# A triangle multiplication and a gated pair layer on one core: held pieces of b by channels eight apart, two output projections among the last products, the last block's factors on GpSimd

## The chip, the core and the metric

One NeuronCore of a Trainium2 chip runs the whole kernel. The metric is the device time of the program in microseconds (us); its time is the median of several executions. Engines are named as the profile names them: PE is the tensor engine (PEld its weight loads), DVE the vector engine, ACT the scalar engine, POOL is GpSimd, SP the engine whose queue issues most of the DMAs.

## The reference

Two layers over x of 384 x 384 positions with 128 channels, all in float32:

```python
# layer 0: triangle multiplication
z_n = layernorm(z)
a = linear(z_n, Wa, ba) * sigmoid(linear(z_n, Wga, bga))
b = linear(z_n, Wb, bb) * sigmoid(linear(z_n, Wgb, bgb))
x = einsum('bijd,bjkd->bikd', a, b)       # for each channel d a 384x384x384 product
x = layernorm(x)
pair = z + linear(x, Wo, bo) * sigmoid(linear(z_n, Wgo, bgo))
# layer 1: gated pair layer
left = pair @ W_left + b_left + (pair @ W_eq + b_eq)
right_sum = sum(pair @ W_right + b_right, over axis 2)
out = left * right_sum * sigmoid(pair @ W_gate + b_gate)
y = layer_norm(out @ W_out + b_out + pair)
```

## The kernel before

The schedule is manual: each engine's queue runs its instructions in the order in which the program writes them, so the order of the Python code is the order of the work. Tiles come from pools with a fixed number of buffers; an instruction that takes a buffer waits until its last readers are done. There are three stages, which hand their data on through DRAM.

**Stage 1, projections (to 1396.9 us).** The positions are cut into 72 tiles of 128 rows by 16 columns, and each tile into 4 steps of 4 columns. A step normalises z (ACT L160, with factors that POOL works out by a power of -0.5, L149), transposes it (zT), and makes a (pa, pga) and b (pb, pgb) with the channels on the partitions; a goes to DRAM array A from POOL's queue (L267), b to B from SP's queue. The output gate is projected by `gate_project` (PE L211 into pgo; DVE L213 adds the bias into one of three gs buffers; ACT L198, in `gate`, takes the sigmoid into one of two gt buffers; POOL issues the store to G, L201). The gate projections of the last 16 steps are put off to the end of the stage. The normalised input's residual Z is stored by POOL (L171 and its DMA). The last 64 columns of b for the last 128 rows are not stored at once: they stay in the SBUF tile `b_held` (channel = partition, 128 rows, 64 columns).

**Stage 2, products (1396.9 to about 2148 us).** For each channel d, `fetch` loads A[d] and B[d] (SP, L470) six channels ahead, `multiply` makes three blocks of 128 rows of the product in PSUM (tile pm, PE L488), and `product` takes the difference to channel 0 (DVE L500, xd), its square (ACT L505, sq), the sums s1 (POOL L507) and s2 (DVE L481), and stores xd to X (SP L508). `store_held` writes 16 channels of `b_held` at a time to B from SP's queue (L476): the first piece ahead of the first full loads, the second right after the loads of the first six channels, and the other six in the course of the stage. A few passes of products that do not need the held columns (`EARLY`) are done at once. The last 8 channels (`LAST`) are done block by block, so that the factors of a block's layer norm can be worked out by `deviation(ib)` between the next block's products: ACT L424, L428 and L432, DVE L426, L427, L430 (a reciprocal), L433, L435 and L437, then three transposes on PE (L443) and a copy on ACT (L444) into `rs0`. `deviation` is a generator, and `advance` runs it one step on. For the last block there is no next block: two steps of it run right after the last product and the others between the first rows of stage 3, the transposes (`pr_last`) in the pass u = 6.

**Stage 3, rows (to the end).** A loop over u writes the work of several rows per pass, each stage of the pipeline with a lag: `load(u+8)` in groups of four rows (xr from X, gr from G, zr from Z, all on SP's queue, L410 to L412), `gate_product(u-3)` (DVE L580), `turn(u-2)` (three transposes, PE L566 into ptr; ACT L568 copies to pairT), `out_weights(u-7)` (ACT L574), `layer_1(u-8)` (PE L592, pf), `layer_0(u)` (PE L602, py; DVE L608 multiplies by factors and gate, L615 adds zr and gives pair; DVE L613 and L618 take the statistics of row u-8), `norm_factors(u-12)` (POOL L625, L626 a power, L628, L629, once in four rows), `normalise(u-13)` (ACT L635), `project(u-2)` (PE L643 pleft and L645 pg; ACT L650 sigmoid; PE L656 once in four rows) and `store(u-17)` (POOL L674 and L675 on four rows at once, then the output's DMA).

## Time and profile before

| | us |
|---|---|
| median of 3 runs | 3340.28 (3338.49 to 3342.46) |
| the profiled execution | 3343.24 |
| its span, first to last instruction | 3341.5 |
| PE busy | 3293.7 (99%) |
| DVE, ACT, POOL busy | 2666.1, 2311.3, 2091.9 |
| mean granted clock of PE | 0.994 |

The profile is of one execution. PEclk is the clock granted to PE, as a share of full speed. A line number such as L488 is that of the code below. In a line of a timeline the bracket at the end gives how long the engine had stood idle, and which instruction's end released it.

### The profile page before, as it was taken

What the parts mean: (1) busy time and instruction counts of PE and PEld (TensorE: products, weight loads), DVE (VectorE), ACT (ScalarE), POOL (GpSimd) and SP (SyncE); (2) the same over time, 40 slices, a digit from 0 to 9 for tenths busy, and PEclk for the clock granted to TensorE, in tenths of its full rate; (3) what the DMA queues carried; (4) which work ended last, traced back from release to release, by engine and by line L of the source; (5) the groups of instructions that cost most, each with busy time, mean ns of one, the idle gap of its engine ahead of it and who ended that gap; (6) DMA issues with size and microseconds to landing.
All of it is one profiled execution on the core that took longest, in us unless ns stands there. A gap on an engine that the chain in (4) does not pass through costs nothing.

```text
span 3341.5 us, 53397 instructions
## 1 busy us (share of the span) xinstructions
PE 3293.7 (99%) x15581; PEld 2191.3 (66%) x15581; DVE 2666.1 (80%) x8599; ACT 2311.3 (69%) x5488; POOL 2091.9 (63%) x1574
## 2 busy tenths in 40 slices
PE   8999999999999999999999999999999999999997
PEld 5555555555555555555555555588888888888885
DVE  8877777777777777455555555799999999999998
ACT  7778787877777788522222222378888888888887
POOL 7555555555555555355555555358888888888887
PEclk9999999999999999999999999999999999999998
DMA  6889899889888889899999999767777777777774
GB/s 226 265 256 273 278 282 282 278 279 281 280 269 264 268 275 282 254 337 318 312 315 311 312 311 304 258 231 262 261 263 262 262 262 264 264 263 263 263 265 142
DMA packets 675522, 910.52 MB, mean 272 GB/s; under 512 B 319520, under 2 KB 616480, under 8 KB 647712
## 3 DMA queue, kind: packets, MB, share of 16 engines
q1 hardware_dynamic: 634192, 680.28, 63.9%
q0 software_dynamic: 40320, 226.51, 19.3%
q8 instruction: 126, 2.06, 0.2%
q14 instruction: 164, 1.34, 0.1%
q10 hardware_dynamic: 720, 0.33, 0.0%
HBM read 454.04 MB, written 452.98 MB: 271 GB/s over the span
## 4 chain that ended last, share of the span: by engine, by line
PE 96%; DVE 2%; POOL 1%; DMA 1%; ACT 0%; issue 0%; POOLq 0%; ACTq 0%; SPq 0%; DVEq 0%
PE pm L488 22%; PE pga L246 8%; PE pa L246 7%; PE pgb L246 7%; PE pb L246 7%; PE py L602 7%; PE pf L592 7%; PE pgo L211 7%; PE pleft L643 7%; PE pg L645 7%; PE ptr L180 4%; PE ptr L566 4%; DMA G<-gt 0%; DVE py L608 0%; PE pg L656 0%
## 5 line engine op out<-in xcount | busy, mean ns | idle before, releaser
L488 PE MATMUL pm<-ab 128*128 128x384 f32 x2304 | 746.6, 487 | 5.8 <-DVE gs L213 5.8
L488 PEld LDWEIGHTS pm<-ab 128*128 128x128 f32 x2304 | 438.9, 191 | 312.4 <-DVE gs L213 6.7
L507 POOL TENSOR_TENSOR acc<-acc,xd 128x384 f32<-128x384 f32 x381 | 380.1, 998 | 362.4 <-DVE xd L500 362.2
L505 ACT ACTIVATE sq<-xd 128x384 f32<-128x384 f32 x381 | 188.5, 495 | 542.3 <-DVE xd L500 542.2
L276 DVE SCALAR_TENSOR_TENSOR bt<-pb,c_L_conv_bb,sgb 128x512 f32<-128x512 f32 x288 | 320.9, 1114 | 243.3 <-ACT zT L191 218.6
L160 ACT ACTIVATE zn<-xt,off,rstd 128x128 f32<-128x128 f32 x1152 | 503.3, 489 | 2.9 <-POOL off L151 2.8
L635 ACT ACTIVATE res<-res,off,rs 128x128 f32<-128x128 f32 x1152 | 482.5, 486 | 18.4 <-POOL off L629 15.7
L500 DVE TENSOR_TENSOR xd<-pm,acc 128x384 f32<-128x384 f32 x381 | 212.2, 557 | 343.3 <-POOL acc L507 321.3
L608 DVE SCALAR_TENSOR_TENSOR py<-py,acc,gr 128x128 f32<-128x128 f32 x1152 | 433.7, 377 | 2.2 <-PE py L602 1.6
L267 POOL DMA_DIRECT2D A<-at x72 | 85.4, 1186 | 539.2 <-DVE at L263 539.2
L251 ACT ACTIVATE sga<-pga,c_L_conv_bga 128x512 f32<-128x512 f32 x288 | 197.9, 687 | 267.6 <-PE pga L246 267.6
L211 PEld LDWEIGHTS pgo<-wT_go,zT 128*128 128x128 f32 x2176 | 285.7, 192 | 130.0 <-issue 66.5
L613 DVE BATCH_NORM_STATS2 st<-res 128x6 f32<-128x128 f32 x1152 | 361.4, 315 | 0.3
L675 POOL TENSOR_TENSOR res<-res,r_L_conv_ln_bias 128x1536 f32<-128x1536 f32 x94 | 324.6, 3453 | 7.4
L171 POOL TENSOR_TENSOR acc<-xt,r_L_conv_b_out 128x2048 f32<-128x2048 f32 x72 | 327.4, 4548 | 1.8
L592 PE MATMUL pf<-w_o,h 128*128 128x128 f32 x2304 | 321.2, 276 | 6.1 <-ACT w_o L574 5.3
L674 POOL TENSOR_TENSOR res<-res,r_L_conv_ln_scale 128x1536 f32<-128x1536 f32 x94 | 325.3, 3461 | 0.2 <-issue 0.2
L650 ACT ACTIVATE sg<-pg,c_L_conv_b_gate 128x384 f32<-128x384 f32 x384 | 223.0, 581 | 144.5 <-PE pg L645 92.6
L602 PE MATMUL py<-w_o,xr 128*128 128x128 f32 x2304 | 321.1, 276 | 0.0
L643 PE MATMUL pleft<-pairT,m_L_conv_W_left 128*128 128x384 f32 x768 | 313.1, 489 | 2.8 <-ACT pairT L568 2.8
L645 PE MATMUL pg<-pairT,m_L_conv_W_gate 128*128 128x384 f32 x768 | 311.1, 487 | 0.0
L141 DVE BATCH_NORM_STATS2 st<-xt 128x6 f32<-128x128 f32 x1152 | 305.5, 265 | 3.7 <-DMA xt<-in_x_dram 3.6
(142 smaller groups left out, 6826.8 us busy)
## 6 DMA issues: line engine op xcount, KB each, us to landing
A<-at POOLq DMA_DIRECT2D x72, 1024.0 KB, 8.5
Z<-acc POOLq DMA_DIRECT2D x72, 1024.0 KB, 8.2
G<-gt POOLq DMA_DIRECT2D x72, 1024.0 KB, 9.2
xr<-X SPq DMA_DIRECT2D x96, 768.0 KB, 6.0
gr<-G SPq DMA_DIRECT2D x96, 768.0 KB, 7.6
zr<-Z SPq DMA_DIRECT2D x96, 768.0 KB, 8.8
X<-xd SPq DMA_DIRECT2D x381, 192.0 KB, 6.2
xt<-in_x_dram SPq DMA_DIRECT2D x71, 1024.0 KB, 17.9
```

The source lines that it names most:

```text
L160: nc.scalar.activation(g["zn"][:, c, :], g["x"][:, c, :], AF.Identity, bias=g["off"][:, c : c + 1], scale=g["rstd"][:, c : c + 1],)
L211: nc.tensor.matmul(pgo[:, c, :], lhsT=zT[:, c, :], rhs=wT["go"], start=True, stop=True)
L246: nc.tensor.matmul(pk, lhsT=wT[k], rhs=zT, start=True, stop=True)
L488: nc.tensor.matmul(products[d, ib], lhsT=ab[:, 0, q, ib * P : (ib + 1) * P], rhs=ab[:, 1, q, :], start=(q == 0), stop=(q == NB - 1),)
L507: nc.gpsimd.tensor_tensor(s1[:, ib, :], s1[:, ib, :], xd, ALU.add)
L592: nc.tensor.matmul(pf[:, q, :], lhsT=h[:, q * P : (q + 1) * P], rhs=w_o, start=True, stop=True)
L602: nc.tensor.matmul(py[:, q, :], lhsT=g["x"][:, i, q * P : (q + 1) * P], rhs=w_o0, start=True, stop=True)
L608: nc.vector.scalar_tensor_tensor(py[:, q, :], py[:, q, :], rs0[:, q, u : u + 1], g["g"][:, i, q, :], ALU.mult, ALU.mult)
L613: nc.vector.bn_stats(b["st"][:, k, q, :], b["res"][:, k, q, :])
L635: nc.scalar.activation(g["res"][:, i, q, :], g["res"][:, i, q, :], AF.Identity, bias=g["off"][:, i, q : q + 1], scale=g["rs"][:, i, q : q ...
L643: nc.tensor.matmul(pleft, lhsT=w_left, rhs=pairT, start=True, stop=True)
L645: nc.tensor.matmul(pg[:, 0:N], lhsT=w_gate, rhs=pairT, start=True, stop=True)
```

## The change

There are three parts.

1. The channels are taken in the order 0, 8, 16, ..., 120, 1, 9, ...: `order[d]` is the channel that is loaded and stored at place d. `store_held` writes the 16 channels k, k+8, ..., k+120 of `b_held`, so a piece stands on partitions eight apart instead of on 16 adjacent ones.
2. `load` is split into `load_pair` (gr, zr) and `load_x` (xr). For the first eight rows `load_pair` is issued among the last products of the second block, and `load_x` at the beginning of the last block. `layer_0(0)` and `layer_0(1)` are written after the third last and the second last product, with py in one of stage 2's pm banks. The row loop begins at u = 2.
3. The factors of the last block are made by `last_deviation` on POOL: five operations on 128 x 384, then the power of -0.5 in 48 pieces of 128 x 8, then a product for X and the transposes. One step is written in each pass for u = 2 to 11, and from then on one in each pass with u % 4 = 1: pieces to u = 181, the product and its store at u = 185, the transposes at u = 189. Rows 256 and on use these factors. DVE's and ACT's operations of `deviation` are left for the first two blocks.

```diff
-    def deviation(ib, bank):
+    def load_x(u):
+        xr = pl.tile([P, R, N], FP, tag="xr", name=f"xr_{u}")
+        u1 = u % P
+        nc.sync.dma_start(out=xr, in_=X[u // P][:, u1 : u1 + R, :])
+        group[u // R]["x"] = xr
...
+    def deviation(ib):
...
+    def turn_factors(ib, r, pr):
         for q in range(NB):
             nc.tensor.transpose(pr[:, q * P : (q + 1) * P], r[:, q * P : (q + 1) * P], ident)
         nc.scalar.copy(rs0[:, :, ib * P : (ib + 1) * P], pr.rearrange("p (q i) -> p q i", q=NB))
+
+    def last_deviation(ib, bank):
+
+        v, t, r = (work_of.tile([P, N], FP, tag="w" + k, name=f"{k}_{ib}") for k in "vtr")
+        nc.gpsimd.tensor_tensor(t, s1[:, ib, :], s1[:, ib, :], ALU.mult)
+        yield
+        nc.gpsimd.tensor_scalar(t, t, -1.0 / (C * C), None, ALU.mult)
+        yield
+        nc.gpsimd.tensor_scalar(v, s2[:, ib, :], 1.0 / C, None, ALU.mult)
+        yield
+        nc.gpsimd.tensor_tensor(v, v, t, ALU.add)
+        yield
+        nc.gpsimd.tensor_scalar(v, v, 0.0, EPS, ALU.max, ALU.add)
+        yield
+        W = 8
+        for k in range(0, N, W):
+            nc.gpsimd.tensor_tensor(r[:, k : k + W], v[:, k : k + W], mhalf[:, 0:W], ALU.pow)
+            yield
+        nc.gpsimd.tensor_tensor(t, v, r, ALU.mult)
+        nc.sync.dma_start(out=X[ib][0], in_=t)
+        yield
+        turn_factors(ib, r, bank())
...
+        order = [d for k in range(C // HELD) for d in range(k, C, C // HELD)]
...
-                    out=factors[d][:, k, q0:q1], in_=of[d, q0 * P : q1 * P].rearrange("(q p) i -> p q i", p=P)
+                    out=factors[d][:, k, q0:q1],
+                    in_=of[order[d], q0 * P : q1 * P].rearrange("(q p) i -> p q i", p=P),
...
-        def store_held(d):
-            if d < C:
-                nc.sync.dma_start(out=B[d : d + HELD, N - P :, N - CG :], in_=b_held[d : d + HELD])
+        def store_held(i):
+            if i < C:
+                k = i // HELD
+                nc.sync.dma_start(out=B[k :: C // HELD, N - P :, N - CG :], in_=b_held[k :: C // HELD])
...
-            nc.sync.dma_start(out=X[ib][d], in_=xd)
+            nc.sync.dma_start(out=X[ib][order[d]], in_=xd)
...
         for ib in range(NB):
-            if ib == NB - 1:
-                load(0)
-                load(R)
             for d in range(C - LAST, C):
+                if ib == NB - 1 and d == C - LAST:
+                    load_x(0)
+                    load_x(R)
                 product(d, ib)
                 if behind:
                     advance(behind)
+                if ib == NB - 2 and d in (C - LAST, C - LAST + 1):
+                    load_pair((d + LAST - C) * R)
+                if ib == NB - 1 and d in (C - 3, C - 2):
+                    layer_0(d + 3 - C, -1, lambda u: pp2.tile([P, N], FP, tag="pm", name=f"py_{u}").rearrange(
+                        "p (q c) -> p q c", q=NB
+                    ))
             add_squares()
-            behind = deviation(
-                ib, lambda b: pt2.tile([P, N], FP, tag="pr", name=f"pr_{b}")
-                if b < NB - 1 else pp.tile([P, N], FP, tag="ptr", name="pr_last")
-            )
-        advance(behind, 2)
+            behind = deviation(ib) if ib < NB - 1 else None
...
-        for u in range(N + stages[-1][1]):
+        load(2 * R)
+        behind = last_deviation(NB - 1, lambda: pp.tile([P, N], FP, tag="ptr", name="pr_last"))
+        for u in range(2, N + stages[-1][1]):
             for stage, lag in stages:
                 if stage is layer_0:
-                    stage(u, u - 8)
+                    stage(u, u - 8, lambda u: pyp.tile([P, NB, C], FP, tag="py", name=f"py_{u}"))
                 elif 0 <= u - lag < N or (stage is last_right and u - lag == N):
                     stage(u - lag)
-            advance(behind)
+            if u < 12 or u % R == 1:
+                advance(behind)
```

More of the change, by code (lines that the diff above doesn't have):

```diff
@@ L405, in load, with load_pair @@
             return
-        xr = pl.tile([P, R, N], FP, tag="xr", name=f"xr_{u}")
+        load_pair(u)
+        load_x(u)
+    def load_pair(u):
         zr = pl.tile([P, R, NB, C], FP, tag="zr", name=f"zr_{u}")
         gr = pl.tile([P, R, NB, C], FP, tag="gr", name=f"gr_{u}")
-        u1 = u % P
-        nc.sync.dma_start(out=xr, in_=X[u // P][:, u1 : u1 + R, :])
         nc.sync.dma_start(out=gr, in_=G[u : u + R].rearrange("i (p q) c -> p i q c", q=NB))
         nc.sync.dma_start(out=zr, in_=Z[u : u + R].rearrange("i (p q) c -> p i q c", q=NB))
-        g = {"x": xr, "z": zr, "g": gr}
+        g = {"z": zr, "g": gr}
         g["total"] = pl.tile([P, R], FP, tag="total", name=f"total_{u}", bufs=4)
@@ L416, in load, with of, layer_0 @@
         group[u // R] = g
-    def deviation(ib, bank):
+    def load_x(u):
[3 more added lines that the diff above has]
+        group[u // R]["x"] = xr
+    def of(u):
+        return group[u // R], u % R
+    pairs = {}
+    def layer_0(u, v, bank):
+        now, past = 0 <= u < N, 0 <= v < N
+        if now:
+            g, i = of(u)
+            py = bank(u)
+            for q in range(NB):
+                nc.tensor.matmul(
+                    py[:, q, :], lhsT=g["x"][:, i, q * P : (q + 1) * P], rhs=w_o0, start=True, stop=True
+                )
+            pairs[u] = pairs_of.tile([P, NB, C], FP, tag="pair", name=f"pair_{u}")
+        for q in range(NB):
+            if now:
+                nc.vector.scalar_tensor_tensor(
+                    py[:, q, :], py[:, q, :], rs0[:, q, u : u + 1], g["g"][:, i, q, :], ALU.mult, ALU.mult
+                )
+            if past:
+                b, k = of(v)
+                nc.vector.bn_stats(b["st"][:, k, q, :], b["res"][:, k, q, :])
+        if now:
+            nc.vector.tensor_tensor(pairs[u], py, g["z"][:, i], ALU.add)
+        if past:
+            for q in range(NB):
+                nc.vector.bn_aggr(b["mv"][:, k, q, :], b["st"][:, k, q, :])
+    def deviation(ib):
         def work(k):
@@ L440, in deviation @@
         yield
-        pr = bank(ib)
+        turn_factors(ib, r, pt2.tile([P, N], FP, tag="pr", name=f"pr_{ib}"))
+    def turn_factors(ib, r, pr):
         for q in range(NB):
@@ L532 @@
         pl = ctx.enter_context(tc.tile_pool(name="p3l", bufs=3, reuse_waits="tile"))
+        pairs_of = ctx.enter_context(tc.tile_pool(name="p3r", bufs=12, reuse_waits="tile"))
         behind = None
         for ib in range(NB):
-            if ib == NB - 1:
-                load(0)
-                load(R)
             for d in range(C - LAST, C):
+                if ib == NB - 1 and d == C - LAST:
+                    load_x(0)
+                    load_x(R)
                 product(d, ib)
@@ L556 @@
     ) as pp:
-        pairs, hs, wos = {}, {}, {}
-        def of(u):
-            return group[u // R], u % R
+        hs, wos = {}, {}
         def turn(u):
@@ L593, in layer_1 @@
             nc.vector.tensor_tensor(g["res"][:, i], pf, pairs.pop(u), ALU.add)
-        def layer_0(u, v):
-            now, past = 0 <= u < N, 0 <= v < N
-            if now:
-                g, i = of(u)
-                py = pyp.tile([P, NB, C], FP, tag="py", name=f"py_{u}")
-                for q in range(NB):
-                    nc.tensor.matmul(
-                        py[:, q, :], lhsT=g["x"][:, i, q * P : (q + 1) * P], rhs=w_o0, start=True, stop=True
-                    )
-                pairs[u] = ps.tile([P, NB, C], FP, tag="pair", name=f"pair_{u}", bufs=12)
-            for q in range(NB):
-                if now:
-                    nc.vector.scalar_tensor_tensor(
-                        py[:, q, :], py[:, q, :], rs0[:, q, u : u + 1], g["g"][:, i, q, :], ALU.mult, ALU.mult
-                    )
-                if past:
-                    b, k = of(v)
-                    nc.vector.bn_stats(b["st"][:, k, q, :], b["res"][:, k, q, :])
-            if now:
-                nc.vector.tensor_tensor(pairs[u], py, g["z"][:, i], ALU.add)
-            if past:
-                for q in range(NB):
-                    nc.vector.bn_aggr(b["mv"][:, k, q, :], b["st"][:, k, q, :])
         def norm_factors(u):
```

## The prediction, written before the changed kernel had run

> **What bounds the kernel now.** First the busy times and the chain of waits of the whole page.

> ```profile
> PE 3293.7 (99%) x15581; PEld 2191.3 (66%) x15581; DVE 2666.1 (80%) x8599; ACT 2311.3 (69%) x5488; POOL 2091.9 (63%) x1574
> ...
> PE 96%; DVE 2%; POOL 1%; DMA 1%; ACT 0%; issue 0%; POOLq 0%; ACTq 0%; SPq 0%; DVEq 0%
> ```

> TensorE is busy 3293.7 of 3341.5 us and holds 96% of the chain that ended last. An edit can shorten the run only where PE stands idle or runs below full clock. Taking the span window by window (columns: length, then PE, PEld, DVE, ACT, POOL busy with counts, PEclk, DMA share, GB/s), I find three such places: the two borders between stages, and the last 40 us.

> ```profile
> 1383.00:1387.00 4.00, 4.00 (x38) 4.00 (x37) 3.04 (x6) 2.85 (x5) 0.30 (x1) 1.00 0.93 248
> 1387.00:1391.00 4.00, 4.00 (x38) 4.00 (x37) 3.19 (x5) 2.19 (x4) 0.81 (x2) 1.00 0.60 77
> ...
> 1403.00:1407.00 4.00, 4.00 (x7) 2.19 (x8) 0.69 (x1) 2.19 (x4) 0.93 (x2) 0.50 1.02 353
> ```
> ```profile
> 2150.00:2160.00 10.00, 4.26 (x12) 3.06 (x13) 8.79 (x18) 4.16 (x8) 1.02 (x2) 0.64 0.99 345
> 2160.00:2170.00 10.00, 9.53 (x44) 6.84 (x42) 7.87 (x18) 3.66 (x10) 0.00 (x0) 0.85 0.42 137
> ...
> 2500.00:2560.00 60.00, 60.00 (x391) 48.70 (x390) 60.00 (x241) 52.80 (x146) 49.37 (x31) 1.00 0.77 264
> ```

> The stretch 2500-2560 stands for stage 3: PE and DVE both full, POOL not. The timeline at the border of stages 1 and 2 (start, us, engine, line, [idle before <-releaser]) names the cause:

> ```profile
> 1399.53 2.19 ACT L198 ACTIVATE gt<-gs 128x512 f32<-128x512 f32 x4 [9.55 <-DMA G<-gt]
> 1400.19 2.48 DVE L213 TENSOR_TENSOR gs<-pgo,r_L_conv_bgo 128x512 f32<-128x512 f32 x4 [8.19 <-ACT gt L198]
> ...
> 1402.73 1.65 PE L488 MATMUL pm<-ab 128*128 128x384 f32 x2 [5.77 <-DVE gs L213]
> ```

> A product needs a PSUM bank that DVE's gate addition (L213) empties; that waits for a gs buffer, released by ACT's sigmoid (L198); that waits for a gt buffer, released when a G store lands. The two G stores were issued at 1386.70 and 1390.27 and took up to 12.8 us; the page's median for G is 9.2. Beside them only 77 GB/s moved, with the first held store on SP's queue (issued 1382.62, landed 14.9 us later). PE loses 5.77 us idle, and then until about 1408.65 works at PEclk 0.50: nine passes at 0.64 instead of 0.32 us, 2.9. **Together 8.7 us.**

> At the border of stages 2 and 3:

> ```profile
> 2154.21 2.54 DVE L430 RECIPROCAL r<-sg 128x384 f32<-128x384 f32 x1
> ...
> 2154.35 0.90 PE L566 MATMUL ptr<-ident,pair 128*128 128x128 f32 x3 [4.67 <-DVE pair L615]
> ...
> 2156.78 0.52 ACT L432 ACTIVATE t<-r 128x384 f32<-128x384 f32 x1 [3.53 <-DVE r L430]
> 2157.21 0.56 ACT L568 ACTIVATE pairT<-ptr,c_L_conv_b_out 128x384 f32<-128x384 f32 x1
> ...
> 2157.92 1.65 PE L643 MATMUL pleft<-pairT,m_L_conv_W_left 128*128 128x384 f32 x2 [1.39 <-ACT pairT L568]
> ```

> PE waits 4.67 us for the first pair. Then the last block's factors stand ahead of the rows: ACT waits for the reciprocal, and PE for ACT, 1.39. PE is at half clock till about 2162.9; ptr of row 2 comes at 2164.09.

> [...] The held piece is 64 floats = 256 bytes a row[...] the trace shows G slow there, not why.[...]

> **The change, part by part.**

> (1) Held pieces eight apart. A piece has the same 2048 rows of 256 bytes[...] The G stores come free that much earlier and the first lands near 1396 instead of 1399.5; the page's median for G says the same (1386.70 + 9.2 = 1395.9). PE resumed 3.2 us after that landing (ACT, DVE, PE in a row), which gives 1399.1. Its own work lasts until 1396.96, so it waits some 2.2 us; the bank that follows the second landing may add 0.5[...].[...] **Gain 8.7 - 2.2 = 6.5** (5.5 to 8; 3.6, the idle alone, if the clock drops all the same; 0 if the store is not faster). Its later pieces go out during stage 2, where PE is full and loads have six channels of lead: nothing. The channel order alone moves no work: A and B loads, products and X stores are the same in number and size.

> (2) Rows 0 and 1 early. py_0 and py_1 (six passes, 1.5 us) move from after the last product into the last three, PE's total unchanged. Their DVE work goes ahead of the last xd: 3 x 0.38 + 0.56 each. Pair 0 is ready about 2150.0, pair 1 about 2152.6. The first transpose's PSUM bank, however, is freed by the addition of squares of the last product but one, which now stands behind these: about 2153.65. So PE's idle stays near 4.1 us, and I take the clock drop as happening (85%). What does go is the reciprocal chain (L426 to L437), and with it the 1.39 us before pleft. From ptr_0 to ptr_1 6.29 - 1.39 = 4.9 us at half clock: ptr_1 at 2158.55. The other restart was at half clock for 5.9 us, so mine ends near 2159.6, and ptr_2, in the chain of 2.79 us a row seen right after, comes at 2161.0 instead of 2164.09. **Gain 3.1** (2.4 to 3.7; 1.5 if half clock lasts as long as before; 5.2 with no drop). The early g and z loads go on SP's queue during the second block's last products; xr for rows 0 to 7 stays before the last block (issued 2134.56, py_0 needs it at about 2144, an xr load takes 6.0): nothing. pr_last with its 1.21 us of PE (0.49 and 0.71 idle on ACT's copy) moves from row 6 to row 189: nothing net.

> (3) The last factors on GpSimd. Rows 2 to 11 take five prelude operations and five pow pieces of 128x8; POOL is at 0.00 in 2160-2170: nothing. The other 43 pieces go one to a group of four rows, rows 13 to 181. What POOL has there:

> ```profile
> L675 POOL TENSOR_TENSOR res<-res,r_L_conv_ln_bias 128x1536 f32<-128x1536 f32 x6 | 20.7, 3453 | 0.5
> L674 POOL TENSOR_TENSOR res<-res,r_L_conv_ln_scale 128x1536 f32<-128x1536 f32 x5 | 17.3, 3461 | 0.0
> L626 POOL TENSOR_TENSOR rs<-rs,mhalf 128x12 f32<-128x12 f32 x5 | 11.5, 2298 | 0.4
> ...
> L625 POOL TENSOR_SCALAR rs<-mv 128x12 f32<-128x12 f32 x5 | 1.2, 248 | 9.0 <-DVE mv L618 9.0
> ```

> A group takes 12.01 us (4 x 2.96 and one L656). POOL's six operations with gaps take 10.3; it waits 9.0/5 = 1.8 before L625. The same pow at 128x8 appears in stage 1 (L149) at 1.67 us, with a gap 1.75: 12.05 against 12.01. POOL falls behind by about 0.04 a group, 43 x 0.04 = 1.7 us at the most; its reader, ACT's L635, waited on POOL only 15.7 us in the whole run, so ACT has slack of its own. **Loss 0.3** (0 to 4). DVE, full here, is not slowed by a busier POOL: L608 took 3 x 0.38 with POOL idle at 2165 and 377 ns on the mean of all rows. DVE's six operations of the last factors are those that (2) takes away; no new wait is put on DVE or ACT, and at row 189 on PE only pr_last's.

> **Sum:** -6.5 - 3.1 + 0.3 = -9.3. The profiled execution took 3343.24 us (span 3341.5), 2.96 above the median 3340.28; 3343.24 falls to 3333.9, the median to **3331.0**. About 0.2%, 6.7 us, is what a measurement of this kernel can tell from no change.

> **Rivals.** *The held store is no faster*[...]. For: 2048 packets of 256 bytes either way, and DMA share is 0.60, not full, while they go.[...] Gain 3.1 - 0.3: 3340.28 - 2.8 = 3337.5, no change to be told. This is also the case that the change does not do what it says. *The clock drops at both borders although PE waits less*: part 1 gives 3.6, part 2 1.5: 3340.28 - 4.8 = 3335.5.[...] *No drop anywhere*: 8.0 + 5.2 - 0.3: 3327.4.[...] against: 4.67 dropped it. *GpSimd becomes the bound of rows 13 to 181*: slower. Each group grows by what a piece exceeds 1.7 us; the price is 43 times the excess, and the point is 0.38 us: 43 x 0.38 = 16.3 eats the 9.6 of the other parts and 6.7 more. A piece of 2.2 us gives 43 x 0.5 = 21.5, so 3340.28 - 9.6 + 21.5 = 3352.2. For: the margin of 0.05 us is nil, and PE, DVE and POOL would all be full. Against: 1.67 is measured on this operation and shape.

> **Chances.** Forecast 0.50, drop at both 0.10 (all of it within 0.2%), no drop 0.10, store no faster 0.18, GpSimd 0.12. Faster: 0.50 + 0.10 = 0.60; same 0.10 + 0.18 = 0.28; slower 0.12. The range runs from just under the best case, 3326.0, to 3345, which takes in the store's failure together with a loss of 4 on GpSimd (3341.2) and the mild end of the slower case; the rest of that, under 0.12, is left out.

> **What would show it.** Right: over 120 GB/s in the windows that had 77, G landing in about 8 us, PE's wait among the first products about 2 us and PEclk never at 0.5 there; ptr of row 0 about 0.7 us earlier, pairT of row 0 right behind it; L625's wait near nothing in rows 13 to 181 and rows still 12.0 us in four; an idle of 0.7 us near row 189. Wrong: G still landing after 12 us; a group of 12.4 us while the pieces run; PE's idle at the second border over 5 us.

## The result and the profile after

The changed kernel takes 3332.67 us (median of 11 runs, 3331.92 to 3333.19); the kernel before, beside it, 3341.18 (11 runs, 3338.49 to 3343.26). The ratio is 0.9975, with a 95% interval of 0.9968 to 0.9983: 8.5 us faster. The prediction said 3331.0, 9.3 us faster. The profiled execution has a span of 3330.9 us against 3341.5 before, 10.6 less; some 2 us of that are the kernel before's own, whose profiled execution (3343.24) lies 2.1 above its median.

The page of the changed kernel, busy times and chain of waits:

```profile
PE 3289.1 (99%) x15581; PEld 2188.5 (66%) x15581; DVE 2661.4 (80%) x8593; ACT 2309.9 (69%) x5485; POOL 2178.3 (65%) x1628
...
PE 97%; DVE 1%; POOL 1%; ACT 0%; DMA 0%; issue 0%; POOLq 0%; ACTq 0%; DVEq 0%
```

PE has the same 15581 instructions and 4.6 us less busy time, which fits passes that ran at half clock before and run at full clock now. POOL's busy time rose by 86.4 us, and the span did not follow it. Code lines have moved: L488 is now L554, L566 is L632, L568 is L634, L643 is L684, L625 is L666.

**The first border.** Windows of the changed kernel (length, busy PE, PEld, DVE, ACT, POOL, PEclk, DMA share, GB/s), then its timeline:

```profile
1387.00:1391.00 4.00, 4.00 (x38) 4.00 (x37) 2.99 (x6) 2.52 (x4) 0.86 (x2) 1.00 0.82 202
...
1399.00:1403.00 4.00, 4.00 (x12) 2.23 (x13) 0.69 (x1) 2.17 (x4) 1.12 (x2) 1.00 1.03 379
```
```profile
1387.13 0.56 POOL L201 DMA_DIRECT2D G<-gt  x1 [4.73 <-ACT gt L198]
...
1395.72 2.19 ACT L198 ACTIVATE gt<-gs 128x512 f32<-128x512 f32 x4 [5.31 <-DMA G<-gt]
...
1398.92 23.34 PE L554 MATMUL pm<-ab 128*128 128x384 f32 x71 [1.54 <-DVE gs L213]
```

Where 77 GB/s moved, 202 do. G's first store, issued at 1387.13, lets the sigmoid go at 1395.72, 8.6 us later; before, it was 12.8. The first held store itself lands after 9.7 us instead of 14.3. PE idles 1.54 us instead of 5.77, and after that PEclk is 1.00, not 0.50. In this execution the border costs 1.54 instead of 8.7 us.

**The second border.** Timeline of the changed kernel:

```profile
2147.13 0.90 PE L632 MATMUL ptr<-ident,pair 128*128 128x128 f32 x3 [4.02 <-DVE acc L547]
...
2148.07 0.58 ACT L634 ACTIVATE pairT<-ptr,c_L_conv_b_out 128x384 f32<-128x384 f32 x1 [0.52 <-PE ptr L632]
...
2149.11 1.28 PE L684 MATMUL pleft<-pairT,m_L_conv_W_left 128*128 128x384 f32 x2
...
2150.87 0.49 PE L632 MATMUL ptr<-ident,pair 128*128 128x128 f32 x3
```

PE still idles 4.02 us ahead of the first transpose, and the releaser is as predicted the addition of squares (L547), not the pair. The first transposes run at half clock (0.90 for three); pairT follows directly, pleft waits for nothing, and the next transposes at 2150.87 are at full clock (0.49). I measure this border from the end of the work that both orders have done by then (products, pr, py of rows 0 and 1) to the first transpose of row 2: 2149.68 to 2164.09 before, 14.4 us; 2143.11 to 2153.66 after, 10.55. That is 3.9 us less.

**The rows.** POOL's groups in 2500-2560 of the changed kernel (count, busy, mean ns, idle before):

```profile
L500 POOL TENSOR_TENSOR r<-v,mhalf 128x8 f32<-128x8 f32 x5 | 8.3, 1670 | 0.0
...
L666 POOL TENSOR_SCALAR rs<-mv 128x12 f32<-128x12 f32 x5 | 1.3, 257 | 0.8 <-DVE mv L453 0.8
```

A piece takes 1670 ns, and the wait for DVE fell from 9.0 to 0.8 us in five groups. PE is busy 60.00 of 60.00 in this window, as before. From ptr of row 2 to the last instruction it is 1177.4 us before (2164.09 to 3341.5) and 1177.2 after (2153.66 to 3330.9), so the pieces cost the rows nothing. At row 189 the predicted 0.71 us is there: the transpose behind pr_last has `[0.71 <-ACT acc L483]`, as row 6 had.

### The profile page after: what moved, and what is told of

Same layout as the page of the kernel before. It is cut to its first block, busy times and chain, and to the rows that moved or that the text cites. A ratio compares the mean times of both kernels' runs of the same rounds, so it can differ in the third digit from the quotient of the medians.

```text
span 3330.9 us, 53440 instructions
## 1 busy us (share of the span) xinstructions
PE 3289.1 (99%) x15581; PEld 2188.5 (66%) x15581; DVE 2661.4 (80%) x8593; ACT 2309.9 (69%) x5485; POOL 2178.3 (65%) x1628
## 4 chain that ended last, share of the span: by engine, by line
PE 97%; DVE 1%; POOL 1%; ACT 0%; DMA 0%; issue 0%; POOLq 0%; ACTq 0%; DVEq 0%
PE pm L554 22%; PE py L437 8%; PE pf L658 8%; PE pga L246 8%; PE pleft L684 7%; PE pg L686 7%; PE pa L246 7%; PE pgb L246 7%; PE pb L246 7%; PE pgo L211 7%; PE ptr L632 4%; PE ptr L180 4%; PE pg L697 0%; DMA G<-gt 0%; POOL rs L667 0%
## 5 line engine op out<-in xcount | busy, mean ns | idle before, releaser
L554 PE MATMUL pm<-ab 128*128 128x384 f32 x2304 | 744.1, 486 | 1.5 <-DVE gs L213 1.5
L554 PEld LDWEIGHTS pm<-ab 128*128 128x128 f32 x2304 | 437.3, 190 | 306.4 <-DVE gs L213 2.7
L676 ACT ACTIVATE res<-res,off,rs 128x128 f32<-128x128 f32 x1152 | 482.3, 486 | 14.3 <-POOL off L670 11.4
L566 DVE TENSOR_TENSOR xd<-pm,acc 128x384 f32<-128x384 f32 x381 | 212.1, 557 | 340.9 <-POOL acc L573 321.3
L443 DVE SCALAR_TENSOR_TENSOR py<-py,acc,gr 128x128 f32<-128x128 f32 x1152 | 395.9, 344 | 2.3 <-PE py L437 1.6
L691 ACT ACTIVATE sg<-pg,c_L_conv_b_gate 128x384 f32<-128x384 f32 x384 | 223.2, 581 | 148.2 <-PE pg L686 97.0
L448 DVE BATCH_NORM_STATS2 st<-res 128x6 f32<-128x128 f32 x1152 | 323.7, 282 | 0.3
L437 PE MATMUL py<-w_o,xr 128*128 128x128 f32 x2304 | 320.7, 275 | 0.0
L684 PE MATMUL pleft<-pairT,m_L_conv_W_left 128*128 128x384 f32 x768 | 312.6, 489 | 1.8 <-ACT pairT L634 1.8
```

What stands on the lines that cost most here:

```text
L437: nc.tensor.matmul(py[:, q, :], lhsT=g["x"][:, i, q * P : (q + 1) * P], rhs=w_o0, start=True, stop=True)
L443: nc.vector.scalar_tensor_tensor(py[:, q, :], py[:, q, :], rs0[:, q, u : u + 1], g["g"][:, i, q, :], ALU.mult, ALU.mult)
L554: nc.tensor.matmul(products[d, ib], lhsT=ab[:, 0, q, ib * P : (ib + 1) * P], rhs=ab[:, 1, q, :], start=(q == 0), stop=(q == NB - 1),)
L676: nc.scalar.activation(g["res"][:, i, q, :], g["res"][:, i, q, :], AF.Identity, bias=g["off"][:, i, q : q + 1], scale=g["rs"][:, i, q : q ...
L684: nc.tensor.matmul(pleft, lhsT=w_left, rhs=pairT, start=True, stop=True)
```

## The experiments

Each was timed beside the kernel before, and the ratio is to that. Where two changed kernels were not timed side by side, their kernels before differ by up to 1.2 us (medians 3340.14 to 3341.38), so a difference of about 1 us between them is not told. Where a text says "from the end of pr and py to ptr of row 2", it is the stretch just defined.

**Part 1 alone**, on the kernel before:

```diff
+        order = [d for k in range(C // HELD) for d in range(k, C, C // HELD)]
...
-                nc.sync.dma_start(out=B[d : d + HELD, N - P :, N - CG :], in_=b_held[d : d + HELD])
+                k = d // HELD
+                nc.sync.dma_start(out=B[k :: C // HELD, N - P :, N - CG :], in_=b_held[k :: C // HELD])
```

> Only the held pieces eight apart with the channel order that they need; rows and last factors as before. Theory ([...]PE neither idles long nor loses its clock at the border of stages 1 and 2): 7 us faster than before, ratio about 0.9979; the first G store after the held one lands within 9 us instead of 12.8, PE's idle among the first products 1.5 us, PEclk never 0.5 there. If it is also the clock drop of this border that makes the times of the kernel before scatter over 5 us, the times of this one lie within 2 us. Rival (the gain of the changed kernel comes from the rows and the factors): within 1 us of before.

Measured: 3335.79 us against 3341.38, ratio 0.9982 (0.9975 to 0.9990): 5.6 us. G lands after 8.3 to 9.4 us, and PE idles 1.86 us with PEclk 1.00 behind it:

```profile
1398.07 14.30 PE L491 MATMUL pm<-ab 128*128 128x384 f32 x43 [1.86 <-DVE gs L213]
```

So part 1 by itself mends the first border. Its times lie within 2.4 us (14 runs), those of the kernel before beside it within 5.8 (56 runs): a little more than expected, and not proof that this clock drop makes the scatter.

**Parts 2 and 3 without part 1**: the changed kernel with

```diff
-        order = [d for k in range(C // HELD) for d in range(k, C, C // HELD)]
+        order = list(range(C))
...
-                nc.sync.dma_start(out=B[k :: C // HELD, N - P :, N - CG :], in_=b_held[k :: C // HELD])
+                nc.sync.dma_start(out=B[i : i + HELD, N - P :, N - CG :], in_=b_held[i : i + HELD])
```

> Rows 0 and 1 early and the last factors on GpSimd; held pieces on adjacent partitions and channels in their own order. Theory: the first border is as before (5.8 us idle, half clock for 6 us), the second gives what it gave in the changed kernel, 3.9 us: ratio about 0.9988. Rival (the two borders are not independent, the second one's half clock being short only because the first had moved the work): 2 us or less.

Measured: 3338.16, ratio 0.9989 (0.9983 to 0.9996): 3.2 us. G's landing is up to 12.1 us again and PE idles 5.13. With part 1's 5.6 the two make 8.8, against 8.5 for the whole: the borders add up. The stretch at the second border is 11.6 us here, 10.55 in the whole change, with the same idle of 4.02; counted from PE's restart, half clock lasts 5.9 us here and 2.9 there. The code of this border is the same in both; the last section shows where the difference comes from.

**Part 2 alone**: as the run before, with the last block's factors by `deviation` on ACT and DVE:

```diff
-        behind = last_deviation(NB - 1, lambda: pp.tile([P, N], FP, tag="ptr", name="pr_last"))
...
-            if u < 12 or u % R == 1:
-                advance(behind)
+            advance(behind)
```

> Only rows 0 and 1 early; the last block's factors by ACT and DVE between the first rows, as before. Theory (the reciprocal chain is what holds ACT and DVE after the last product): ptr of row 0 comes 0.7 us earlier after the last product, but the chain now falls on rows 2 to 4 and takes 1 to 2 us of PE there, so the gain is 1 to 2.5 us. Rival (early rows are what matters): all 3.9 us.

Measured: 3340.97, ratio 0.9996 (0.9987 to 1.0004): 0.4 us, no change that can be told, and less than the 1 to 2.5 expected. The first transpose comes with the same idle of 4.02, but then the chain of the last factors takes its place. Timeline of part 2 alone (L614 transposes, L666 pleft, L616 pairT here):

```profile
2151.07 0.55 PE L614 MATMUL ptr<-ident,pair 128*128 128x128 f32 x3 [4.02 <-DVE acc L525]
...
2154.47 1.65 PE L666 MATMUL pleft<-pairT,m_L_conv_W_left 128*128 128x384 f32 x2 [2.18 <-ACT pairT L616]
...
2162.22 0.91 PE L666 MATMUL pleft<-pairT,m_L_conv_W_left 128*128 128x384 f32 x2 [0.65 <-ACT pairT L616]
```

PE waits 2.18 us for pairT, where the kernel before waited 1.39, and loses a little more two rows on.

**Part 3 alone**: rows 0 and 1 as before, the last factors on GpSimd:

```diff
-            behind = deviation(
-                ib, lambda b: pt2.tile([P, N], FP, tag="pr", name=f"pr_{b}")
-                if b < NB - 1 else pp.tile([P, N], FP, tag="ptr", name="pr_last")
-            )
-        advance(behind, 2)
+            behind = deviation(ib, lambda b: pt2.tile([P, N], FP, tag="pr", name=f"pr_{b}")) if ib < NB - 1 else None
...
+        behind = last_deviation(NB - 1, lambda: pp.tile([P, N], FP, tag="ptr", name="pr_last"))
...
-            advance(behind)
+            if u < 12 or u % R == 1:
+                advance(behind)
```

> Only the last block's factors on GpSimd in pieces; rows 0 and 1 after the last product, as before. Theory: without L426 and L427 ahead of it row 0's L608 starts right behind the last addition of squares, about 1.5 us earlier, PE idles some 3.1 us instead of 4.67, pairT follows at once (1.39 us less), so a gain of 2.9 us, and up to 5 if PE keeps its clock with 3.1 us idle. GpSimd's pieces cost nothing in the rows. Rival (the early rows do the work): 1.4 us or less. Rival of a full GpSimd: slower than before by up to 4 us, and groups of four rows over 12.1 us.

Measured: 3336.51, ratio 0.9985 (0.9978 to 0.9991): 4.9 us, more than parts 2 and 3 together. Timeline of part 3 alone (L589 transposes, L666 pleft):

```profile
2150.75 0.90 PE L589 MATMUL ptr<-ident,pair 128*128 128x128 f32 x3 [2.97 <-DVE pair L638]
...
2152.72 1.18 PE L666 MATMUL pleft<-pairT,m_L_conv_W_left 128*128 128x384 f32 x2
...
2154.39 0.49 PE L589 MATMUL ptr<-ident,pair 128*128 128x128 f32 x3
```

The idle is 2.97, a microsecond less than with the early rows, and the stretch to ptr of row 2 is 9.4 us (2147.77 to 2157.18). The clock is halved here too, for 2.7 us after the restart. So the gain at this border is part 3's, and the early rows take some of it back.

**Parts 1 and 3 without the early rows**: the two diffs above together.

> Parts 1 and 3: held pieces apart and the last factors on GpSimd; rows 0 and 1 stay after the last product. Theory (the early rows put their DVE work ahead of the last differences and so delay the first transpose by about 1 us more than they save): the gains measured apart add up, 5.6 + 4.9 = 10.5 us, 3330.9, and so 1 to 2 us faster than the whole change; PE idles 3.0 us before the first transpose, not 4.0. Rival (the runs of the factors alone were lucky ones): as the whole change, 3332.7, or slower by the 0.7 us that ptr comes later.

Measured: 3331.10, ratio 0.9970 (0.9959 to 0.9982), 9.7 us faster than before and 1.6 faster than the whole change's 3332.67 (1.2 if each is set against the kernel before beside it). The expected 3330.9 came out, with 2.96 us of idle and a stretch of 9.5 us to ptr of row 2.

**Two apart instead of eight.** The changed kernel with channels 0, 2, ..., 30, then 1, 3, ..., 31 and so on:

```diff
+        order = [b + k + 2 * j for b in range(0, C, 2 * HELD) for k in range(2) for j in range(HELD)]
...
+                b = k // 2 * 2 * HELD
+                ks = slice(b + k % 2, b + 2 * HELD, 2)
+                nc.sync.dma_start(out=B[ks, N - P :, N - CG :], in_=b_held[ks])
```

> The whole change, but the 16 channels of a held piece stand two apart (0, 2, ..., 30) and not eight[...]. Theory[...]: as the whole change within 1 us, G's first store lands in 8 to 9 us, over 200 GB/s in the four us after it is issued. Rival (it is the distance between partitions, or how far the rows lie apart in DRAM): G's landing moves back towards 12 us, PE idles 4 us or more, up to 7 us slower than the whole change.

Measured: 3331.63, ratio 0.9973 (0.9962 to 0.9983). G lands in 6.6 to 9.4 us; 181 GB/s in 1387-1391, a little under the 200 expected, then 390; idle 0.89. A distance of two does as well here as one of eight (3332.67 and an idle of 1.54).

**Eight channels four apart in either half of the partitions, in two DMAs**: the changed kernel with

```diff
+        order = [h + b + k + 4 * j for b in (0, 32) for k in range(4) for h in (0, P // 2) for j in range(HELD // 2)]
...
+                b = k // 4 * 32 + k % 4
+                for h in (0, P // 2):
+                    ks = slice(h + b, h + b + 2 * HELD - 3, 4)
+                    nc.sync.dma_start(out=B[ks, N - P :, N - CG :], in_=b_held[ks])
```

> The whole change, but a held piece has 8 channels four apart in either half of the partitions, in two DMAs[...]. Theory[...]:[...] G's first store lands in 7 to 8 us, PE's idle among the first products falls from 1.5 to under 0.8 us: 0.5 to 1.5 us faster than the whole change. Rival[...]: the same idle of 1.5 us and the same time within 0.5 us.

Measured: 3330.81, ratio 0.9969 (0.9957 to 0.9980), 1.9 us faster than the whole change. Its window and PE's timeline:

```profile
1387.00:1391.00 4.00, 4.00 (x39) 4.00 (x38) 2.99 (x6) 2.52 (x4) 0.79 (x2) 1.00 0.91 312
...
1396.00 6.29 PE L557 MATMUL pm<-ab 128*128 128x384 f32 x19
```

G lands in 5.0 to 7.2 us, and PE's idle is gone. Time, landing and idle came out a little better than expected, but two things were changed at once: the distance between the channels and the number of DMAs. So the second was run alone.

**Eight apart, but in two DMAs**: the changed kernel with

```diff
+                for h in (0, P // 2):
+                    ks = slice(h + k, h + P // 2, C // HELD)
+                    nc.sync.dma_start(out=B[ks, N - P :, N - CG :], in_=b_held[ks])
```

> The whole change, with each held piece stored in two DMAs, channels k to k+56 and k+64 to k+120, still eight apart[...]. Theory[...]: as the whole change, 3332.7 within 1 us, an idle of about 1.5 us among the first products, some 200 GB/s in 1387-1391. Rival[...]:[...] 3330.8, no idle, over 280 GB/s.

Measured: 3337.56, ratio 0.9990 (0.9982 to 0.9999), 4.9 us slower than the whole change. Both expectations were wrong. PE's timeline with two DMAs eight apart:

```profile
1397.44 1.56 PE L556 MATMUL pm<-ab 128*128 128x384 f32 x4 [0.34 <-DVE gs L213]
1402.37 23.00 PE L556 MATMUL pm<-ab 128*128 128x384 f32 x66 [3.37 <-DVE gs L213]
```

The first G store lands in time, the second only after 10.5 us, and PE idles 3.37 us for that one. Counting in the traces the 256-byte packets of the first held piece that start in each microsecond, from that of its first packet on (which can hold only a part of one; 2048 in all), shows how the pieces went:

```
adjacent (before)             40 306 303 302 300 297 256  98  88  35  22   1
eight apart (part 1 alone)   216 752 717 285  71   7
two apart                    156 650 599 531 111   1
four apart, two DMAs           2 493 524  28  24 255 554 168
eight apart, two DMAs        260 331 280 106  50  47 154 148 124 198 211  44   8  63  24
```

In one DMA some 300 packets of adjacent channels start in a microsecond, which is 77 GB/s; eight or two apart it is 600 to 750, which is 154 to 192 GB/s. The last two rows differ only in the distance: the same two DMAs of eight channels and the same packets. Four apart, either DMA reaches 500 and more. Eight apart, the first DMA reaches 260 to 331, the second 124 to 211, beside G's packets. So neither the distance nor the number of DMAs alone explains the rates: eight apart is fast with sixteen channels in one DMA and slow with eight in each of two. What does explain them was not shown.

The two DMAs do not run at once: each row of two has two bursts. So the 312 GB/s of the window from 1387 to 1391 with pieces four apart are not those of two halves side by side.

What the held piece does to G shows in the same traces. G is issued some 0.4 us after the piece's first packet in each of them. Its own first large packet starts 5.7 us after its issue beside the adjacent piece, 2.2 beside the piece eight apart in one DMA, 2.9 two apart, 1.4 four apart in two DMAs, 1.2 eight apart in two. With the adjacent piece not one large packet of any queue starts from 1387.5 to 1391.5: G does not go slowly there, it waits. With four apart in two DMAs, the two microseconds between the bursts move 393 and 417 KB in large packets: the first G store goes between the halves of the piece. Eight apart in two DMAs, the second half and the second G store run beside each other, and from 1393 to 1397 both are slow: 124 to 211 packets of the piece and 33 to 172 KB of G in a microsecond. So a piece in two DMAs helped four apart, where the bursts lasted some 2 and 3 us, and hurt eight apart, where they lasted some 4 and 9.

**A full GpSimd**: `W = 16` for `W = 8` in the changed kernel.

> The whole change with pieces of 128x16 instead of 128x8: 24 pieces, 5 in passes 7 to 11 and 19 in groups of four rows. A piece of that size takes 2.94 us in stage 1, so GpSimd has 13.3 us of work in a group of 12.01. Theory (a group grows by what GpSimd has too much, once its slack is used up): 19 x 1.28 = 24 us less 3 to 5 us of slack, so about 20 us slower than the whole change, 3352; L666 no longer waits for DVE, and PE waits in the groups in which pieces run. Rival (GpSimd's lateness is hidden by buffers): within 3 us of the whole change.

Measured: 3352.82, ratio 1.0036 (1.0023 to 1.0048), 20.2 us slower than the whole change: the price of the slower rival, and it was priced right. Waits of this run, by engine (us, times, longest; PE in 2180-2450, ACT in 2300-2400), and a window of it:

```profile
PE pleft L684 <- ACT pairT L634: 15.7, 18, 0.9
...
ACT res L676 <- POOL off L670: 12.1, 7, 1.7
```
```profile
2300.00:2400.00 100.00, 92.77 (x592) 74.32 (x591) 92.08 (x362) 80.45 (x224) 97.04 (x52) 1.00 0.68 235
```

In this window POOL no longer waits for DVE at all. Its factors come late, ACT's normalise waits for them, pairT stands behind that on ACT, and PE waits for pairT, once in a group, up to 0.9 us each. From ptr of row 2 to the last instruction it is 1197.5 us, 20.3 more than in the whole change.

**A mended version**: pieces four apart in two DMAs, last factors on GpSimd, row 1 behind the last product, and another layout of stage 3's PSUM banks:

```diff
-                if ib == NB - 1 and d in (C - 3, C - 2):
-                    layer_0(d + 3 - C, -1,
+                if ib == NB - 1 and d in (C - 3, C - 1):
+                    if d == C - 1:
+                        add_squares()
+                    layer_0((d + 3 - C) // 2, -1,
...
+        pfp, pp, pyp, plp, pgp = (
+            ctx.enter_context(tc.tile_pool(name=n, bufs=b, space=PSUM, reuse_waits="tile"))
+            for n, b in (("p3f", 2), ("p3p", 1), ("p3y", 2), ("p3pl", 2), ("p3pg", 1))
+        )
```

(pf, pleft and pg take their tiles from pfp, plp and pgp.)

> [...]last factors on GpSimd, and the early rows mended: row 0 after the third last product as in the change, row 1 behind the last one and behind its additions of squares; PSUM pools of stage 3 set out so that the first transpose takes the bank of the last product but one and pleft, pg and py banks that are free by then. Theory (the first transpose waited for DVE's queue, not for its own data): ptr of row 0 within 1 us of PE's last pass, PE's longest idle there about 2 us[...]; from the end of pr and py to ptr of row 2 7.7 us instead of 10.5: 2.8 us faster[...], 3328.0. Rival (pairT or the activation table load then holds PE as long): 1 us faster or less.

Measured: 3327.10 (3326.68 to 3327.65), ratio 0.9959 (0.9946 to 0.9971): 13.5 us faster than the kernel before, 5.8 faster than the changed kernel beside it, 3.7 faster than with the two DMAs four apart alone, where 2.8 was expected. Its timeline (L639 transposes, L691 pleft):

```profile
2141.45 0.55 PE L639 MATMUL ptr<-ident,pair 128*128 128x128 f32 x3 [0.98 <-DVE xd L569]
...
2143.88 0.91 PE L691 MATMUL pleft<-pairT,m_L_conv_W_left 128*128 128x384 f32 x2 [1.21 <-ACT pairT L641]
...
2145.27 0.49 PE L639 MATMUL ptr<-ident,pair 128*128 128x128 f32 x3
```

Two short idles, 0.98 and 1.21, in place of one of 4.02, and no half clock: from 2140.47 to ptr of row 2 at 2148.06 it is 7.6 us. With the two DMAs four apart alone that stretch was 11.4 us in its profile (2141.20 to 2152.59), with half clock for 4.9 us after the restart, longer than in the whole change; the 3.8 between the two stretches fits the 3.7 that were timed. The 1.21 left is a wait for pairT, as the rival said, but a short one; the activation table load (1.28 us) starts at 2143.84, when pairT is done. Row 1's place and the PSUM banks were changed together, so what either gives is not known.

**Parts 1 and 3 with pieces four apart in two DMAs**, without early rows:

> Parts 1 and 3 without the early rows[...]. Theory (the borders add up): no idle among the first products, 3.0 us before the first transpose: 1.3 us faster than parts 1 and 3[...], 3329.8. Rival: no different from 3331.1.

Measured: 3329.34, ratio 0.9965 (0.9952 to 0.9977), 1.8 us under the same with pieces eight apart in one DMA. The borders add up here too. In its profiled execution the clock was not halved at the second border, although PE idles as long as in part 3 alone:

```profile
2143.75 0.55 PE L595 MATMUL ptr<-ident,pair 128*128 128x128 f32 x3 [2.97 <-DVE pair L644]
```

The mended version beats it by 2.2, so early rows can be worth something once their DVE work does not stand ahead of the last differences.

**The whole change again**, beside the last two:

> The whole change once more, beside the two others on one chip: 3332.7 within 1 us, ratio 0.9975, if the differences of 1 to 2 us between runs of different calls are those of the kernels; nearer 3331 if they are those of the chip.

Measured: 3332.86, ratio 0.9976 (0.9966 to 0.9985). It comes within 0.2 us of the first median (3332.67), as expected if the differences of 1.5 us and more are those of the kernels.

## Why the prediction was right

**The first border** went as written. The held store left earlier (9.7 us; 14.3 before, where the prediction's 14.9 is a median with a later piece), G's first landing came after 8.6 us (9.2 was used), PE's idle was 1.54 (2.2), and the clock held. That the piece would go faster eight apart was the author's estimate; the traces show it going faster (some 700 packets in a microsecond against 300), not why. That G waits behind the held store, which the prediction could not read from its lines, is shown by the packets of the traces. 6.5 us were predicted; 7.1 is what the two profiles give (5.77 - 1.54, and the 2.9 of half clock), 5.6 what the timed run of part 1 gives. The second is the better measure of the median: the profiled execution of before had an idle of 5.77 and a half clock of 6.8 us on the record, while three other runs with the same first border had idles of 4.4 to 5.1, and two of them a half clock of some 3.4. So the border was priced from one of its costlier executions. That the clock would hold at the 2.2 us of idle was not shown by any trace then; it held at 1.54, and 2.97 us dropped it in part 3 alone.

**The second border** came out at 3.9 in the profile and 3.2 in the timed run of parts 2 and 3, against 3.1. Over the seven traces that have this border the stretch is 10.55 to 11.6 us, which is 2.8 to 3.9 less than before. The early part was right: the first transpose 0.65 us sooner, waiting for the addition of squares, an idle of 4.02 for 4.1, the clock halved, the wait for pairT gone. Two terms were off, and one of them was put in the wrong place:
- "mine ends near 2159.6", half clock for 5.9 us as at the other restart: it was 2.9 us in the changed kernel, and 5.9 in the run without part 1, with the same idle. The idle alone does not give the length (last section).
- The sum booked 3.1 to "Rows 0 and 1 early" and a loss of 0.3 to GpSimd. The runs book it the other way: early rows alone 0.4, factors on GpSimd alone 4.9, and without the early rows the change is 1.6 us faster. The prediction did say that it is the reciprocal chain's going that saves PE's wait; but it is part 3 that takes the chain away. It also saw that the early rows' DVE work, 2 x 1.7 us, stands ahead of the last differences and their squares, and so kept the idle near 4.1. What it did not ask is what the border costs without the early rows once the chain is gone: 2.97 us of idle instead of 4.02. That the sum of this border came out is to that extent luck: the terms were booked to the wrong parts.

**GpSimd** cost nothing that can be seen. The piece was sized right (1670 ns against 1.67 us), the margin was nil as predicted, and the rows kept their length (1177.2 us against 1177.4). The rival's rule, that a group grows by what POOL has too much, is supported by the run with pieces of 16 columns: 20.2 us slower, 20 expected. The slack of 3 to 5 us taken there was an estimate and was not measured apart.

The sum, 9.3, is above the 8.5 measured and inside its interval (5.7 to 10.7).

## What to carry to other kernels

A store from sixteen adjacent partitions held up the stores behind it (G's first large packet started 5.7 us after its issue, and 2.2 with the piece eight apart): try partitions that stand apart within one DMA before looking for another place for it, and measure it before keeping it in two DMAs (four apart they gained 1.9 us, eight apart they lost 4.9). When work is moved forward past a border, look at what it is put ahead of on each engine and whose PSUM bank is freed by that; the early rows gained nothing until the second of them was put behind the last differences and the banks were laid out anew. A spare engine was free up to about the length of this loop's period: with an estimated 12.05 of 12.01 us it cost nothing, with 13.3 some 20 us in 19 groups.

## What the runs showed of the hardware

- All five steps at full clock with 2.17 us of idle or more were followed by half clock (3.41, 3.12 and 2.17 before; 3.41 and 2.63 after), and none with 1.54 us or less.
- Ahead of the last 40 us, half clock ended after all three steps with at most 0.50 us of idle, and went on after all three with 0.86 or more (0.86, 1.54 and 1.39).

So in these two traces what goes with the clock is the idle within a step, and with it where the steps fall. Two kernels with the same idle of 2.97 us ahead of the first transpose show it too, each cut into the steps of its own record (length of the step, busy PE, PEld, DVE, ACT, POOL, PEclk, DMA share, GB/s). Part 3 alone:

```profile
2146.64:2150.06 3.42, 1.14 (x11) 0.94 (x9) 3.25 (x8) 1.40 (x3) 2.77 (x3) 1.00 1.04 383
2150.06:2153.47 3.41, 2.72 (x11) 2.42 (x12) 2.60 (x8) 1.77 (x3) 3.16 (x4) 0.50 0.95 285
```

Parts 1 and 3 with pieces four apart in two DMAs:

```profile
2138.89:2142.31 3.42, 1.89 (x16) 1.64 (x14) 3.32 (x7) 1.40 (x3) 2.24 (x4) 1.00 1.06 385
2142.31:2145.72 3.41, 1.88 (x11) 1.51 (x12) 3.16 (x9) 1.37 (x3) 3.16 (x4) 1.00 0.97 299
```

In the first, 2.28 us of idle fell into one step, and the next ran at half clock. In the second the same idle was split, with 1.53 us of idle in either step (0.09 of it from other short waits), and the clock held. The length of half clock goes with the same steps: after the same idle of 4.02 us, the step of the restart had 0.50 us of idle in the whole change and 0.97 in the run without part 1, which stayed at half clock for one step more, to about 2158.4. With part 2 alone the transposes at 2151.07, behind the same 4.02 us, still took the 0.55 us of full clock, and pleft at 2154.47 took 1.65, at half clock. The idles of 0.98, 1.21 and 1.54 us were not followed by half clock, nor was the 1.86 of part 1 alone, of which 0.42 fell into one step and 1.44 into the next. Between 1.54 and 2.17 us of idle in a step the two traces do not tell.
